# Layer 0's second linear in seven block products, and layer 1's first batch without an opening of its own

## The chip, the core and the metric

The kernel runs on one core of a Trainium2 chip. A core has a matrix engine (TensorE, PE in the profile), three engines for vectors (VectorE or DVE, ScalarE or ACT, GpSimd or POOL) and SyncE (SP), which issues the DMAs here. The engines run side by side, each through its own instructions in order, and wait for one another by semaphores. The metric is the device time of one execution in microseconds, median of several runs.

## The reference, cut to what matters

Two layers follow each other on 16 batches of a 1024 x 256 matrix x, in float32:

```python
# layer 0
agg = einsum('nm,bmd->bnd', A_hat, x)              # A_hat: adj + I, scaled by degrees
h   = relu(batchnorm(agg @ W1.T + b1))             # 512 hidden
out = batchnorm(h @ W2.T + b2)                     # the second linear: 512 -> 256
x   = layernorm(x + out)
# layer 1
c   = mean(x, channels)
Wg  = adj * gate(c_i - c_j)                        # per batch, 1024 x 1024
q   = relu((x.T @ Wg) * para);  k, v = split(x @ kv_w)
x   = layernorm(x + attention(q, k, v))            # 4 heads
```

A batch norm needs the mean and variance over all batches, so the second linear can't start before the first has been through all of them, and layer 1 can't start before the second has.

## The kernel before

**Layer 0, up to the second linear.** For each batch, `aggregate` multiplies x by the scaled adjacency (in batches 1 to 15 by seven products of half-size blocks, after Strassen and Winograd, in which GpSimd makes the sums of blocks of x, `sums_x`), and `hidden` gives the 512 hidden channels of its two halves. A *unit* is one half of a batch (512 rows): 32 units, each a tile `hT` of 128 x 4 x 512. The last `KEEP` = 5 stay in SBUF, the others are written to DRAM. The pool `hp` has 9 such tiles. `bn_affine` turns statistics into a scale and a shift (DVE, with two POOL instructions for the root).

**The second linear** (L340 to L389). Units are taken in the order kept ones first. For each, `first` (L350) is four relus on ScalarE in place, `second` (L356) eight matmuls (two output halves c times four k), then for each c `bn_stats` from PSUM on DVE, a copy to `y` on ScalarE, and a DMA of y to `yT` in DRAM. `fetch` reads units from DRAM four ahead. The weights of layer 1 are loaded behind the sixth unit, in one go.

**Layer 1.** A list `at` holds, for each slot, which pieces are issued there. A batch has NC = 8 slots; its attention is 16 steps, four of which follow every two slots (`scores`, `exps`, `sums`, `attend`). Score tiles have two PSUM buffers, so scores wait for the exps of the step before. The pieces around it prepare later batches: two batches ahead `load`, `bn2` (L436: layer 0's second batch norm applied to yT, ScalarE), `ln1_a` (transposes `py`, add x, statistics), `ln1_b`, `x1_t` (transposes `px`, copy), `means`, `crow` (the means as a row on all partitions); one batch ahead the gate tiles `wg_a` and `wg_b`, `keys`, `values`, and `graph` (the products for the queries `q`). `dens`, `recips`, `finish_a` and `finish_b` normalise and write the output of a batch. `finish_b` waits for `nm` from POOL. `arrange` (L772) sorts the pieces of a slot: `dens` and `bn2` first, the gate in pairs, the long products spread between the short pieces, and whatever isn't an instruction of PE behind what ranks before it in `order` (L758).

**The opening of batch 0** (L802 to L876) isn't in that list. It has buffers of its own for tiles 2 and 3 of the four that make up the batch (taken from the pool `ep`), so that all four are loaded at once; applies bn2 and the statistics to all four; normalises on ScalarE (`ln1_b0`); makes keys of the first half before tiles 2 and 3 are transposed; copies keys on DVE; and makes all four query sums side by side in the score tiles (`graph0`), one gate tile after the other, while batch 1 is prepared in the slots beside it.

**The end.** In the last batch `finish_b` of the first half is put late, behind the last step (L720), r tiles come from the pool of x1 (L648), and `range_all` (a check on the softmax denominators) is in slot NC + 1, before the last `finish_a`.

The line that decides the first places in a slot, and the ranks:

```python
        order = (dens, recips, finish_a, finish_b, x1_t, ln1_a, ln1_b, means, load, crow)
...
            first += [fa for fa in pieces if fa[0] is bn2]
```

Of the kernel before, what the change touches and what calls it, by code (L numbers as in the profile page):

```python
# [16 lines left out]
P = 128  # L17
# [5 lines left out]
def gnn_norm_attention_kernel(  # L23
# [62 lines left out]

    with ExitStack() as l0:
# [6 lines left out]
        KEEP = 5  # L94
# [227 lines left out]
        def load_weights():  # L322
            nc.sync.dma_start(kvw, kv_w.rearrange("(c p) f -> p c f", p=P))
            for i in range(0, NT, 2):
                nc.sync.dma_start(
                    adj_sb[:, i : i + 2, :], adj[i * P : (i + 2) * P, :].rearrange("(c p) m -> p c m", p=P)
                )
            nc.sync.dma_start(para_sb, para.rearrange("o (c p) h w -> p c (o h w)", p=P))

        def load(b, j):  # L330
            yts[b, j] = ldp.tile([P, CT, 2 * P], F32, tag="yt", name=f"yt{b}_{j}")
            xrs[b, j] = ldp.tile([P, 2, C], F32, tag="xr", name=f"xr{b}_{j}")
            fetch_rows(b, j)

        def fetch_rows(b, j):
            nc.sync.dma_start(yts[b, j], yT_dram[b][:, :, ts(j, 2 * P)])
            nc.sync.dma_start(xrs[b, j], x[b, ts(j, 2 * P), :].rearrange("(a p) c -> p a c", p=P))


        with ExitStack() as ph2:  # L340
            yp = ph2.enter_context(tc.tile_pool(name="yp", bufs=3))
            ps = ph2.enter_context(tc.tile_pool(name="ps2", bufs=4, space=PSUM, reuse_waits="tile"))

            order = list(range(len(units) - KEEP, len(units))) + list(range(len(units) - KEEP))

            def fetch(u):
                hT[u] = hp.tile([P, HT, FB], F32, tag="h", name=f"hL{u}")
                nc.sync.dma_start(hT[u], h_dram[u])

            def first(u):  # L350
                for f in range(HT):
                    nc.scalar.activation(
                        hT[u][:, f, :], hT[u][:, f, :], AF.Relu, bias=t1[:, f : f + 1], scale=s1[:, f : f + 1]
                    )

            def second(u):  # L356
                b, h = units[u]
                y = yp.tile([P, CT, FB], F32, tag="y", name=f"y{u}")
                po = [ps.tile([P, FB], F32, tag="a", name="po") for c in range(CT)]
                mm = [(c, k) for c in range(CT) for k in range(HT)]  # L360
                if u == order[0]:
                    mm.sort(key=lambda ck: ck[1])
                for c, k in mm:
                    nc.tensor.matmul(  # L364
                        po[c], W2T[:, k, ts(c, P)], hT[u][:, k, :], start=(k == 0), stop=(k == HT - 1)
                    )
                for c in range(CT):
                    nc.vector.bn_stats(st2[:, c, b * NH + h, :], po[c])  # L368
                    nc.scalar.copy(y[:, c, :], po[c])
                    if u == order[-1]:  # L370
                        bn_affine(st2, c, g2t, be2t, b2t, s2, t2, "bn2")
                nc.sync.dma_start(yT_dram[b][:, :, ts(h, FB)], y)
                hT.pop(u)

            AHEAD = 4
            for u in order[KEEP : KEEP + AHEAD]:
                fetch(u)
            for k in range(len(units) + 1):
                if k < len(units):
                    first(order[k])  # L380
                if k > 0:
                    second(order[k - 1])
                    if KEEP + AHEAD + k - 1 < len(units):
                        fetch(order[KEEP + AHEAD + k - 1])
                if k == KEEP:
                    load_weights()
                if k == len(units) - 2:
                    for j in range(LDP):
                        load(0, j)  # L389

# [22 lines left out]
    def fast():  # L413
      with ExitStack() as fx:
# [102 lines left out]
        def keys(b, c, h):  # L517
            if h == 0:
                kTs[b, c] = kp.tile([P, N], F32, tag="kT", name=f"kT_{b}_{c}")
            p = ps_t.tile([P, FB], F32, tag="t", name="pk")  # L520
            for k in range(CT):
                nc.tensor.matmul(  # L522
                    p, kvw[:, k, ts(c, P)], x1Ts[b][:, k, ts(h, FB)], start=(k == 0), stop=(k == CT - 1)
                )
            (nc.vector.tensor_copy if b == 0 else nc.scalar.copy)(kTs[b, c][:, ts(h, FB)], p)
# [16 lines left out]
        def graph(b, m):  # L542

            h, c, k = m // (CT * NT), m // NT % CT, m % NT
            if k == 0:
                pg[b] = ps_t.tile([P, FB], F32, tag="t", name="pg")
            nc.tensor.matmul(  # L547
                pg[b], x1s[b, k // 2][:, k % 2, ts(c, P)], wgs[b, k][:, ts(h, FB)], start=(k == 0), stop=(k == NT - 1)
            )
            if k == NT - 1:  # L550
                queries(b, c, h, pg[b])

        def queries(b, c, h, p):
            qs = qTs[b, c, h] = qp.tile([P, FB], F32, tag="qT", name=f"qT_{b}_{c}_{h}")
            nc.vector.tensor_mul(qs, p, para_sb[:, c, ts(h, FB)])  # L555
            nc.vector.tensor_scalar(qs, qs, 0.0, scale, op0=OP.max, op1=OP.mult)
# [85 lines left out]
        def finish_a(b, j):  # L642
# [5 lines left out]
            pool_r = (rp, "r") if b < B - 1 else (x1p, "x1")  # L648
            r = pool_r[0].tile([P, 2, C], F32, tag=pool_r[1], name=f"r_{b}_{j}")
# [62 lines left out]
        for b in range(B):  # L712

            for hf in range(NH):
# [3 lines left out]
                for k in range(KB // 2):  # L718
                    put(b, t + 1 + k, finish_a, b, hf * (KB // 2) + k)
                    late = NC - t - 2 - k if b == B - 1 and hf == 0 else 0  # L720
                    put(b, t + 2 + k + late, finish_b, b, hf * (KB // 2) + k)
            if b == 0:
                continue

            put(b - 2, 2, begin, b)
            for j in range(NT // 2):
                put(b - 2, j, load, b, j)
# [25 lines left out]
        put(B - 1, NC + 1, range_all)  # L753
# [4 lines left out]
        order = (dens, recips, finish_a, finish_b, x1_t, ln1_a, ln1_b, means, load, crow)  # L758
# [13 lines left out]
        def arrange(pieces):  # L772
# [3 lines left out]
            first += [fa for fa in pieces if fa[0] is bn2]  # L776
# [24 lines left out]

        def ln1_b0(j):  # L802
            mv, rs = mvs.pop((0, j))
            nm = sm.tile([P, 2], F32, tag="nm", name=f"nm_a{j}")
            for a in range(2):
                nc.gpsimd.tensor_scalar(
                    nm[:, a : a + 1], mv[:, a, 0:1], rs[:, a : a + 1], -1.0, op0=OP.mult, op1=OP.mult
                )
            for a in range(2):
                r = x1s[0, j][:, a, :]  # L810
                i = 2 * j + a
                nc.scalar.activation(
                    r, r, AF.Identity, bias=nm[:, a : a + 1], scale=rs[:, a : a + 1], accum_out=css[0][:, i : i + 1]
                )

        def gate0(i):
            wg_a(0, i)
            wg_b(0, i)

        PG0 = []  # L820

        def graph0(k):
            if k == 0:
                PG0.extend(ps_s.tile([P, 2, FB], F32, tag="s", name=f"pg0_{h}") for h in range(NH))
            for h in range(NH):
                for c in range(CT):
                    nc.tensor.matmul(  # L827
                        PG0[h][:, c, :],
                        x1s[0, k // 2][:, k % 2, ts(c, P)],
                        wgs[0, k][:, ts(h, FB)],  # L830
                        start=(k == 0),
                        stop=(k == NT - 1),
                    )
            if k == NT - 1:
                for h in range(NH):
                    for c in range(CT):
                        queries(0, c, h, PG0[h][:, c, :])

        begin(0)
        for j in range(LDP, NT // 2):  # L840
            t = ep.tile([P, 2, FB], F32, tag="e", name=f"first{j}")
            yts[0, j] = t[:, 0, :].rearrange("p (c n) -> p c n", c=CT)
            xrs[0, j] = t[:, 1, :].rearrange("p (a c) -> p a c", a=2)
            fetch_rows(0, j)
        for f in (bn2, ln1_a):
            for j in range(NT // 2):
                f(0, j)
        ln1_b0(0)
        ln1_b0(1)
        x1_t(0, 0)  # L850
        x1_t(0, 1)
        ln1_b0(2)
        ln1_b0(3)
        for c in range(CT):
            keys(0, c, 0)
        x1_t(0, 2)
        x1_t(0, 3)
        means(0)
        crow(0)
        gate0(0)  # L860
        for c in range(CT):
            keys(0, c, 1)
        gate0(1)
        values(0, 0)
        values(0, 2)
        gate0(2)
        values(0, 4)
        values(0, 6)

        def opening(s):  # L870

            k = s + NC
            if 0 <= k < NC:
                for i in range(3 + 2 * k, min(5 + 2 * k, NT)):
                    gate0(i)
                graph0(k)  # L876

        NK = NT // 2  # L880
        for t in range(min(at) // 2, max(max(at) // 2, nsteps // NK - 1) + 1):
            g = NK * t
            now = [p for s in (2 * t, 2 * t + 1) for p in [(opening, (s,))] + arrange(at.get(s, []))]
# [175 lines left out]
```

## Time and profile before

| | us |
|---|---|
| median of 3 runs | 2610.95 (2610.77 to 2611.19) |
| the profiled execution, its time | 2610.95 |
| its span, first to last instruction | 2609.2 |
| layer 0 up to the second linear | 0 to 635 |
| second linear, PE | 635.3 to 857.8 |
| from there to the first scores | 857.8 to 925.2 |
| one batch of layer 1 (scores to scores) | 106.9 |
| the last matmul's start | 2598.0 |

| engine | busy us | share of the span |
|---|---|---|
| PE | 2551.5 | 98% |
| DVE | 1425.5 | 55% |
| ACT | 1217.5 | 47% |
| POOL | 364.0 | 14% |

The profile is of one execution. A line of a timeline gives start, duration, engine, line of the kernel, operation, what it writes and reads, shapes, how many instructions were merged (x), and in brackets how long the engine was idle before and what ended that. A float32 matmul is two instructions in it. A line of the busy time by stretch gives, for each engine, the time in which it ran anything.

### The profile page before, as it was taken

What the parts mean: (1) busy time and instruction counts of PE and PEld (TensorE: products, weight loads), DVE (VectorE), ACT (ScalarE), POOL (GpSimd) and SP (SyncE); (2) the same over time, 40 slices, a digit from 0 to 9 for tenths busy, and PEclk for the clock granted to TensorE, in tenths of its full rate; (3) what the DMA queues carried; (4) which work ended last, traced back from release to release, by engine and by line L of the source; (5) the groups of instructions that cost most, each with busy time, mean ns of one, the idle gap of its engine ahead of it and who ended that gap; (6) DMA issues with size and microseconds to landing.
All of it is one profiled execution on the core that took longest, in us unless ns stands there. A gap on an engine that the chain in (4) does not pass through costs nothing.

```text
span 2609.2 us, 32969 instructions
## 1 busy us (share of the span) xinstructions
PE 2551.5 (98%) x13177; PEld 1117.1 (43%) x13177; DVE 1425.5 (55%) x2250; ACT 1217.5 (47%) x1647; POOL 364.0 (14%) x472
## 2 busy tenths in 40 slices
PE   8999999999999899999999999999999999999997
PEld 4444444444444444444444444444444444443432
DVE  5222222223222465867758667676576775867666
ACT  2111111113555564564655646556465574664644
POOL 1111110100000100211102201111021110211112
PEclk9999999999999899999999999999999999999998
DMA  3222222221863211011000100111000111011000
GB/s 129 81 81 81 97 81 81 81 109 43 315 234 129 81 41 33 25 44 46 25 33 28 55 33 25 34 33 50 33 25 33 34 49 33 25 41 33 9 9 26
DMA packets 93824, 161.65 MB, mean 62 GB/s; under 512 B 7656, under 2 KB 73824, under 8 KB 86752
## 3 DMA queue, kind: packets, MB, share of 16 engines
q1 hardware_dynamic: 93664, 159.48, 17.4%
q8 instruction: 105, 1.72, 0.3%
q14 instruction: 55, 0.45, 0.1%
HBM read 97.53 MB, written 61.93 MB: 61 GB/s over the span
## 4 chain that ended last, share of the span: by engine, by line
PE 91%; ACT 3%; DVE 3%; issue 1%; DMA 1%; POOL 1%; SPq 0%; ACTq 0%; POOLq 0%; DVEq 0%
PE s L573 17%; PE o L604 17%; PE pa L263 14%; PE pg L547 14%; PE po L364 8%; PE ph L284 8%; PE pk L522 4%; PE pv L533 2%; PE pd L625 1%; PE px L472 1%; PE pa L247 1%; PE pg L827 1%; PE pf L647 1%; ACT wg L509 1%; ACT wg L510 1%
## 5 line engine op out<-in xcount | busy, mean ns | idle before, releaser
L585 ACT ACTIVATE e<-s 128x1024 f32<-128x1024 f32 x512 | 496.5, 1021 | 398.7 <-PE s L573 347.2
L594 DVE TENSOR_TENSOR acc<-acc,e 128x1024 f32<-128x1024 f32 x384 | 470.7, 1226 | 88.3 <-ACT e L585 58.6
L573 PE MATMUL s<-qT,kT 64*64 64x512 f32 x4096 | 490.9, 594 | 5.5 <-ACT e L585 4.7
L604 PE MATMUL o<-e,v 64*64 64x512 f32 x4096 | 485.3, 589 | 0.0
L547 PE MATMUL pg<-wg,x 128*128 128x512 f32 x960 | 441.1, 594 | 12.3 <-DVE wg L514 12.3
L303 ACT COPY hT<-ph 128x512 f32<-128x512 f32 x128 | 74.9, 586 | 453.8 <-PE ph L284 453.8
L604 PEld LDWEIGHTS o<-e,v 64*64 64x64 f32 x4096 | 156.7, 133 | 283.5 <-issue 278.5
L573 PEld LDWEIGHTS s<-qT,kT 64*64 64x64 f32 x4096 | 149.8, 133 | 294.8 <-issue 271.2
L547 PEld LDWEIGHTS pg<-wg,x 128*128 128x128 f32 x960 | 168.9, 190 | 176.1 <-issue 149.1
L514 DVE SCALAR_TENSOR_TENSOR wg<-wg,adj_sb 128x1024 f32<-128x1024 f32 x128 | 156.8, 1225 | 127.7 <-ACT wg L510 125.5
L284 PE MATMUL ph<-agg,W1T 128*128 128x512 f32 x512 | 222.2, 592 | 0.0
L66 POOL TENSOR_SCALAR rs_z<-mv_z 128x2 f32<-128x2 f32 x64 | 41.1, 642 | 1036.5 <-DVE mv_z L405 1006.9
L364 PE MATMUL po<-hL,W2T 128*128 128x512 f32 x432 | 185.6, 592 | 0.0
L304 DVE BATCH_NORM_STATS2 st<-ph 128x6 f32<-128x512 f32 x128 | 89.5, 699 | 136.6 <-ACT hT L303 136.6
L263 PE MATMUL pa<-T,sx 128*128 128x512 f32 x360 | 156.9, 592 | 0.0
L284 PEld LDWEIGHTS ph<-agg,W1T 128*128 128x128 f32 x512 | 97.3, 190 | 122.5 <-issue 122.2
L368 DVE BATCH_NORM_STATS2 st<-po 128x6 f32<-128x512 f32 x64 | 44.7, 699 | 169.4 <-PE po L364 169.4
L364 PEld LDWEIGHTS po<-hL,W2T 128*128 128x128 f32 x432 | 82.1, 190 | 103.3 <-issue 103.3
L473 ACT COPY x1T<-px 128x512 f32<-128x512 f32 x64 | 37.1, 581 | 178.5 <-PE px L472 178.5
L533 PE MATMUL pv<-kvw,x1T 128*128 128x256 f32 x512 | 120.1, 379 | 0.0
L522 PE MATMUL pk<-x1T,kvw 128*128 128x512 f32 x256 | 119.0, 609 | 0.7 <-ACT x1T L473 0.7
L555 DVE TENSOR_TENSOR qT<-pg,para_sb 128x512 f32<-128x512 f32 x64 | 43.8, 684 | 128.1 <-PE pg L547 127.1
(144 smaller groups left out, 2619.7 us busy)
## 6 DMA issues: line engine op xcount, KB each, us to landing
h<-hT SPq DMA_DIRECT2D x27, 1024.0 KB, 3.8
hL<-h SPq DMA_DIRECT2D x27, 1024.0 KB, 8.6
x<-in_x_dram SPq DMA_DIRECT2D x16, 1024.0 KB, 5.0
yT<-y SPq DMA_DIRECT2D x32, 512.0 KB, 3.7
out_dram<-r SPq DMA_DIRECT2D x64, 256.0 KB, 2.1
yt<-yT SPq DMA_DIRECT2D x62, 256.0 KB, 3.0
xr<-in_x_dram SPq DMA_DIRECT2D x62, 256.0 KB, 5.0
crow<-crow_d SPq DMA_DIRECT2D x15, 512.0 KB, 4.0
```

The source lines that it names most:

```text
L263: nc.tensor.matmul(p, w[:, k, :], m[:, k, :], start=(k == 0), stop=(k == KN - 1))
L284: nc.tensor.matmul(p, W1T[:, k, ts(f, P)], aggT[b][:, k, ts(h, FB)], start=(k == 0), stop=(k == CT - 1),)
L304: nc.vector.bn_stats(st1[:, f, u, :], p)
L364: nc.tensor.matmul(po[c], W2T[:, k, ts(c, P)], hT[u][:, k, :], start=(k == 0), stop=(k == HT - 1))
L514: nc.vector.scalar_tensor_tensor(t, t, 1.0, adj_sb[:, i, :], op0=OP.add, op1=OP.mult)
L522: nc.tensor.matmul(p, kvw[:, k, ts(c, P)], x1Ts[b][:, k, ts(h, FB)], start=(k == 0), stop=(k == CT - 1))
L533: nc.tensor.matmul(p[:, ts(a, C)], x1Ts[b][:, k, ts(j + a, P)], kvw[:, k, C:], start=(k == 0), stop=(k == CT - 1),)
L547: nc.tensor.matmul(pg[b], x1s[b, k // 2][:, k % 2, ts(c, P)], wgs[b, k][:, ts(h, FB)], start=(k == 0), stop=(k == NT - 1))
L573: nc.tensor.matmul(t[r * HD : (r + 1) * HD, h, :], kTs[b, pair][h * HD : (h + 1) * HD, ts(2 * cb + r, HD)], qTs[b, pair, hf][h * HD : (h + ...
L585: nc.scalar.activation(E[g, a], S.pop((g, a)), AF.Exp)
L594: nc.vector.tensor_add(ACC[b, hf, pair], ACC[b, hf, pair], E[g, a])
L604: nc.tensor.matmul(O[b, hf, pair][r][h * HD : (h + 1) * HD, :], vs[b][r * HD : (r + 1) * HD, cb, pair * P + h * HD : pair * P + (h + 1) * HD],
```

## The change

The second linear is now made for two batches side by side, each by seven products of half-size blocks. With the weights in blocks of (output half, k half) and the hidden units in blocks of (k half, unit), the four sums of weight blocks are made once (`SV`, POOL), and the sums of h blocks in place: one on DVE, three on POOL between the products that read the old value and those that read the new. A generator `seven` issues one product of a batch at a time, and the two batches' generators alternate. What leaves PSUM goes through the running sums u and v: one ScalarE copy and seven DVE additions for a batch, and `bn_stats` reads y in SBUF. The relus of all four kept units are issued before the first product; those of the next pair's units come behind the third to sixth product of a pair. Fetches are for a whole pair, at its start. `KEEP` is 4, PSUM has 8 buffers here, and the weights of layer 1 are loaded over five pairs.

Batch 0 of layer 1 goes through the list `at` like the others: `continue` for b == 0 is gone, only its first two tiles are loaded ahead, and the whole opening is removed. So are the special cases of batch 0's key copies and of the last batch (late `finish_b`, r tiles from x1's pool); `range_all` is one slot later; and `bn2` isn't put first in its slot, but ranks behind `means`.

```diff
+    def seven(product, u, v, out, done=lambda i, j: None):
+        nc.scalar.copy(u, product(1))
+        yield
+        nc.vector.tensor_add(out[0][0], product(2), u)
+        done(0, 0)
+        yield
+        nc.vector.tensor_add(u, product(6), u)
+        yield
+        nc.vector.tensor_add(v, product(7), u)
+        yield
+        nc.vector.tensor_add(out[1][0], product(4), v)
+        done(1, 0)
+        yield
+        p = product(5)
+        nc.vector.tensor_add(out[1][1], p, v)
+        nc.vector.tensor_add(u, p, u)
+        done(1, 1)
+        yield
+        nc.vector.tensor_add(out[0][1], product(3), u)
+        done(0, 1)
+        yield
...
-        KEEP = 5
+        KEEP = 4
...
+            def second(b, final):
+                unit = [b * NH + h for h in range(NH)]
+                (b00, b01), (b10, b11) = ([hT[u][:, i * KF : (i + 1) * KF, :] for u in unit] for i in range(2))
+                bs = {1: b00, 2: b10, 3: b11, 4: b10, 5: b01, 6: b00, 7: b01}
+                nc.vector.tensor_sub(b01, b11, b01)
...
+                def product(n):
+                    p = ps.tile([P, FB], F32, tag="a", name="po")
+                    for k in range(KF):
+                        nc.tensor.matmul(p, ws[n][:, k, :], bs[n][:, k, :], start=(k == 0), stop=(k == KF - 1))
+                    return p
+
+                def done(c, h):
+                    nc.vector.bn_stats(st2[:, c, b * NH + h, :], ys[h][:, c, :])
+                    if final and (c, h) in ((1, 1), (0, 1)):
+                        bn_affine(st2, c, g2t, be2t, b2t, s2, t2, "bn2")
...
+                for k, _ in enumerate(seven(product, u, v, out_q, done)):
+                    if k == 0:
+                        nc.gpsimd.tensor_add(b00, b00, b01)
+                    if k == 1:
+                        nc.gpsimd.tensor_sub(b10, b10, b00)
+                    if k == 3:
+                        nc.gpsimd.tensor_sub(b01, b11, b00)
+                    if k >= 5:
+                        nc.sync.dma_start(yT_dram[b][:, :, ts(k - 5, FB)], ys[k - 5])
...
+            for b in pairs[0]:
+                for h in range(NH):
+                    first(b * NH + h)
+            for k, pair in enumerate(pairs):
+                ahead = [b * NH + h for b in pairs[k + 1] for h in range(NH)] if k + 1 < len(pairs) else []
+                for u in ahead:
+                    fetch(u)
+                load_weights(k)
...
+                gens = [second(b, not ahead and b == pair[-1]) for b in pair]
+                for n in range(7):
+                    for g in gens:
+                        next(g)
+                    if 2 <= n and ahead:
+                        first(ahead.pop(0))
...
-            pool_r = (rp, "r") if b < B - 1 else (x1p, "x1")
-            r = pool_r[0].tile([P, 2, C], F32, tag=pool_r[1], name=f"r_{b}_{j}")
+            r = rp.tile([P, 2, C], F32, tag="r", name=f"r_{b}_{j}")
...
-                    late = NC - t - 2 - k if b == B - 1 and hf == 0 else 0
-                    put(b, t + 2 + k + late, finish_b, b, hf * (KB // 2) + k)
-            if b == 0:
-                continue
+                    put(b, t + 2 + k, finish_b, b, hf * (KB // 2) + k)
...
-        put(B - 1, NC + 1, range_all)
+        put(B - 1, NC + 2, range_all)
...
-        order = (dens, recips, finish_a, finish_b, x1_t, ln1_a, ln1_b, means, load, crow)
+        order = (dens, recips, finish_a, finish_b, x1_t, ln1_a, ln1_b, means, bn2, load, crow)
...
-            first += [fa for fa in pieces if fa[0] is bn2]
...
-        def ln1_b0(j):
...
-        def opening(s):
...
-            now = [p for s in (2 * t, 2 * t + 1) for p in [(opening, (s,))] + arrange(at.get(s, []))]
+            now = arrange(at.get(2 * t, [])) + arrange(at.get(2 * t + 1, []))
```

## The prediction

> **The bound.** The views were read in this order: the page, whose part 1 has PE busy in 98% of the span; the busy time by stretch, to see where the 2% is; and the timelines of PE, ACT, DVE and POOL in one batch of layer 1 and in the tail. By stretch:
>
> ```profile
> core 0: us, PE busy (x) PEld busy (x) DVE busy (x) ACT busy (x) POOL busy (x), PEclk, DMA share, GB/s
> ...
> 672.00:857.70 185.70, 185.70 (x433) 81.89 (x431) 39.45 (x59) 104.98 (x158) 0.79 (x2) 1.00 0.61 222
> 857.70:942.20 84.50, 73.17 (x266) 38.62 (x265) 45.97 (x97) 47.59 (x78) 10.79 (x26) 0.88 0.20 63
> ...
> 1124.90:1231.80 106.90, 105.95 (x701) 45.81 (x705) 73.29 (x116) 61.60 (x79) 17.53 (x24) 1.00 0.11 36
> ```
>
> PE never rests in the second linear (first line), rests 11 us in the opening of layer 1 (second), and 0.95 us in each 106.9 us batch (third). So a matmul saved in the second linear is worth its full price, and anything that makes PE wait once in a batch is paid about fifteen times. The price of a matmul: the chain of waits gives 500 of the instructions of L364 in 214.87 us, 0.4297 us each (two to a matmul).
>
> The batch is tight at two places. ScalarE there (start, duration, line):
>
> ```profile
> 1252.53 1.15 ACT L505 ACTIVATE wg<-crow,hcs 128x1024 f32<-128x1024 f32 x1
> 1253.58 1.08 ACT L439 ACTIVATE yt<-yt,t,s 128x256 f32<-128x256 f32 x2
> 1254.56 0.57 ACT L525 COPY kT<-pk 128x512 f32<-128x512 f32 x1
> 1255.93 0.58 ACT L540 COPY v<-pv 128x512 f32<-128x512 f32 x1 [0.80 <-PE pv L533]
> 1256.41 1.15 ACT L509 ACTIVATE wg<-crow,cs 128x1024 f32<-128x1024 f32 x1
> ...
> 1260.08 1.92 ACT L585 ACTIVATE e<-s 128x1024 f32<-128x1024 f32 x2
> ...
> 1272.47 1.09 ACT L439 ACTIVATE yt<-yt,t,s 128x256 f32<-128x256 f32 x2
> 1273.47 1.08 ACT L668 ACTIVATE r<-r,nm,rs_z 128x256 f32<-128x256 f32 x2
> 1274.45 0.56 ACT L540 COPY v<-pv 128x512 f32<-128x512 f32 x1
> 1274.91 1.15 ACT L509 ACTIVATE wg<-crow,cs 128x1024 f32<-128x1024 f32 x1
> ```
>
> bn2 (L439) of the first tile stands in a gap that ends with a wait of 0.80 for PE; the exps at 1260.08 start with no wait. PE beside it:
>
> ```profile
> 1261.47 1.90 PE L573 MATMUL s<-qT,kT 64*64 64x512 f32 x16
> ...
> 1276.27 0.60 PE L449 MATMUL py<-ident,yt 128*128 128x128 f32 x4
> 1276.71 4.46 PE L547 MATMUL pg<-wg,x 128*128 128x512 f32 x10
> 1282.11 1.12 PE L547 MATMUL pg<-wg,x 128*128 128x512 f32 x2 [0.95 <-DVE wg L514]
> ```
>
> And in the tail, where no graph product covers a late normalisation, a wait of ACT for POOL stops PE:
>
> ```profile
> 2549.89 3.56 PE L573 MATMUL s<-qT,kT 64*64 64x512 f32 x16 [4.13 <-ACT e L585]
> ```
>
> **The skill.** The Trainium skill, "SBUF — State Buffer", Who interferes with whom: a VectorE instruction with two SBUF inputs and a GpSimd instruction that reads SBUF exclude each other[...]. The trace agrees: L66 on POOL takes 0.22 us at 1276.45 with DVE idle, 1.66 at 1262.54 under L591. The Trainium skill, "TensorE: Matmul & The Clock Gate", What's actually happening: after idling the array runs at half rate until it has been busy for a few us. The trace: 8 instructions of L522 take 6.11 us at 875.77, 3.44 at 883.83.
>
> **The change.** The order of instructions on each engine is that of the changed program; durations are from rows of the kernel before.
>
> *Stage 2, PE.* Seven products of 2 matmuls for eight, so 64 of 512 instructions go: 64 x 0.4297 = 27.5 us. 448 take 192.2.
>
> *Stage 2, start.* Before, the matmuls follow the relus one by one: by 642.9 us 12 are done, and 500 follow without a break. In the changed order all 16 relus of the first two batches precede the first copy, and PE alternates batches. Relu 4 starts at 642.03 and each takes 0.705 (5 in 3.63), so the third unit's first two are done at 642.03 + 7 x 0.705 = 647.0. B1 waits for this from 638.5: PE is cold by then (+2.5 us, from L522's pair above). B's subtraction needs relu 16 (651.2) and 1.23 us (L594's shape), then B's first POOL sum. POOL's 128x512 sums start every 1.22 us (L233 to L236), so a 128x1024 sum is taken as 2.4; the Trainium skill's "GPSIMD Engine Reference", Elementwise — side-by-side cycle accounting, has 4497 ns for 2048 elements, an estimate of 2.25. B6 then starts at about 655.9, and the 14 products end at 671.4, 2.5 us of cold clock included. The other 392 instructions: 168.4. End 839.8, where before it was 857.8.
>
> *Stage 2, later pairs.* A pair takes 24.05 us of PE. ACT has 16 relus and 2 copies (12.5), DVE 2 subtractions, 14 additions at 0.62 from start to start and 8 bn_stats at 0.7 (16.7), POOL 6 sums (14.4), DMA 4 MB of h, 2 of y and 1 of weights, 17 us at the 415 GB/s that 692 to 696 us shows. All fit. What is near is POOL's order: VectorE ends the last pair's work 1.7 us into the pair, subtracts for A to 2.9 and for B to 4.0, which blocks A's sum to 4.0 (two SBUF inputs); A's ends at 6.4 (A6 due at 6.9), B's at 8.8 (B6 due at 8.6). I take 0.2 us a pair, 1 us in all; from below 0 (2.25 us a sum), from above 3.5 us a pair, if bn_stats blocked POOL too. Stage 2 ends at 840.8: 17.0 earlier.
>
> *Opening.* Its length, from the end of the second linear to the first key product of batch 1 (927.97), was 70.2. In the changed order:
> bn2's coefficients: VectorE's last four products cost 2 x (2 x 0.62 + 0.7) and 2 x (0.62 + 0.7), and two affines of 2.4 stand among them; it is 3.9 us behind when the last affine starts. Ready at 6.3 instead of 3.2 us.
> Tiles 2 and 3 have no buffers of their own: their loads wait for py of tiles 0 and 1 (8.4, 9.4 us) and for the additions (9.2, 11.0); xr takes up to 5.0 us to land, so tile 2's addition comes at 15.0. Then, a tile at a time: statistics 1.1, ln1_b 0.95, px about 1 at the cold clock. px of tile 3 ends at 24.5, crow at 26.3.
> Keys from there: cold, the first copy at 29.4, and behind it all of ACT's gate work: 8 tiles of 1.05 or 2.15 us, key and value copies, bn2 of batch 1. wg 7 leaves ACT at 50.8 and VectorE at 54.4, so the first query sum is done at 55.3.
> Three more sums: 48 x 0.43 = 20.6, and 2.3 of transposes. First score at 78.2, keys of batch 1 at 80.0.
> So +9.8 us. From below +5 (early loads, warm clock), from above +15.
>
> *bn2 in the batches.* It is no longer put first in its slot. Tile 0's goes from the gap at 1253.58 to behind wg 2: wg 2 still starts at 1256.41, and the exps at 1261.06 instead of 1260.08. The next scores (PE 1261.47) need the buffer that the first exp reads until 1262.08: PE waits 0.7. Tile 1's goes from 1272.47 to behind r, v and wg 4: v still waits for pv (1274.4), wg 4 ends at 1277.0, bn2 at 1278.1. py (1276.27) waits 1.9; the 12 graph instructions take 5.15 from 1278.6 and find wg 5 ready (1281.7), so the 0.95 goes; the scores come at 1283.95 instead of 1283.17, 0.8. Tiles 2 and 3 have time: py at 1301.99 and 1308.89. Together 1.45 us in each of the 13 windows 1 to 13 (in window 0 no output work is ahead of it): +18.9. From below 0, from above 2 a window.
>
> *Tail.* The output normalisations of the last batch's first half run in slots 6 and 7 again, ahead of exps: ACT waits for POOL's nm as at 2547.84 (4.65), PE as above: 4.5 and 1.7 of cold clock, 6.2 less a fraction: +6.0. The range check goes behind the last tile: pf no longer waits for it, and the last addition starts at 2597.4 instead of 2599.16: -1.8. Together +4.2.
>
> Sum on the span: 2609.2 - 17.0 + 9.8 + 18.9 + 4.2 = 2625.1. The profiled execution took 2610.95, 1.75 more than its span, and is the median of the runs. Forecast 2626.9.
>
> **Rivals.**
> *The batches absorb the later bn2* (not slower): ACT idles 45 us in a batch's 106.9, and a wait of 0.7 could vanish if scores had buffers to spare. Against: there are two, and the timeline leaves 0.3 us. Then 18.9 goes: 2608.0. It decides from under 0.5 us a window on.
> *POOL bounds the pairs*: if every VectorE instruction that reads SBUF blocked it, POOL would have 14.4 + 8.1 of 24 us, with waits between that don't overlap; 3.5 us in each of 7 pairs: 2651. Against: POOL's sums of phase 1 all take 1.26 to 1.27 with VectorE's PSUM additions beside them.
> *The opening is longer*, its chain cold throughout, +16 for +9.8: 2633.
> That the products aren't what bounds stage 2 is excluded by the first line above.
>
> **Numbers.** Chances: forecast 0.62, absorbed 0.15, POOL 0.11, opening 0.12. The forecast's own bounds are about 8 us to each side; that is 2619 to 2635; the range reaches over the longer opening and to the middle of the absorbed case, 2608 to 2640, and leaves out POOL and the other half of that case, under 2 in 10. A measurement here can tell 0.2%, 5.2 us. Faster by more: a third of the absorbed case, 0.05. Within: half of it and the forecast's low edge, 0.11. Slower: 0.84.
>
> **The test.** PE's 448 instructions of the second linear ending near 841, with one gap of 8 us at its start; first scores about 78 us later; scores periods of 108.4 where they were 106.9, with waits of PE for e (0.7) and of py for yt (1.9); a second PE wait of about 4.5 us for e, 20 us before the end. It is wrong if the period stays under 107.4, or if pairs last over 25 us.

## The result, and the profile after

The changed kernel takes 2627.26 us (median of 4 runs, 2626.8 to 2628.35), the kernel before 2611.07 beside it: ratio 1.0063, 95% interval 1.0045 to 1.0080. It is 16.2 us slower. The profiled execution took 2627.65 us, its span is 2625.8, 16.6 more than before.

The busy time by stretch, for the changed kernel, with the engines' columns as before:

```profile
core 0: us, PE busy (x) PEld busy (x) DVE busy (x) ACT busy (x) POOL busy (x), PEclk, DMA share, GB/s
671.42:839.70 168.28, 168.28 (x393) 73.84 (x391) 118.41 (x170) 76.55 (x110) 103.81 (x43) 1.00 0.72 278
839.70:922.41 82.71, 62.34 (x202) 33.32 (x201) 42.73 (x108) 31.54 (x48) 11.32 (x20) 0.81 0.17 57
1120.19:1228.40 108.21, 106.44 (x702) 45.69 (x704) 73.32 (x116) 61.94 (x79) 16.35 (x24) 1.00 0.11 35
```

The seven pairs after the first (first line) have no gap in PE at all, 24.03 us a pair. The opening, from the last product to the first key product of batch 1 (second line), is 82.7 us where it was 70.2, with 20 us of rest in it. A batch (third line) lasts 108.21 us for 106.93, with 1.77 us of rest for 0.95.

PE at the start of stage 2:

```profile
634.78 1.12 PE L407 MATMUL po<-hT,W2T 128*128 128x512 f32 x2 [1.39 <-ACT hT L393]
636.23 1.13 PE L407 MATMUL po<-hT,W2T 128*128 128x512 f32 x2 [0.32 <-ACT hT L393]
647.02 7.40 PE L407 MATMUL po<-hT,W2T 128*128 128x512 f32 x12 [9.66 <-ACT hT L393]
```

After the wait of 9.66 us for the relus it runs through to 839.7, 18.0 us before the old end. Half a microsecond of that is not the change's: layer 0 ended earlier in this execution, as the first product of the kernel before shows:

```profile
635.29 3.70 PE L364 MATMUL po<-hT,W2T 128*128 128x512 f32 x8 [1.39 <-ACT hT L352]
```

From its first product (634.78 for 635.29) to its last, the second linear is 17.4 us shorter. The pairs had hardly any time to spare on POOL, though; its sums in one pair:

```profile
674.30 5.53 POOL L419 TENSOR_TENSOR hL<-hL,hL 128x1024 f32<-128x1024 f32 x2 [9.36 <-PE po L407]
679.77 4.70 POOL L421 TENSOR_TENSOR hL<-hL 128x1024 f32<-128x1024 f32 x2
684.41 4.69 POOL L423 TENSOR_TENSOR hL<-hL,hL 128x1024 f32<-128x1024 f32 x2
```

The pair began at 671.42, a product lasts 1.717 us, so the second batch's product 6, the sixth product of the pair, is due at 680.0, and its sum (the second of L419) ends at 679.8.

PE in a batch, at the two places where bn2 comes later:

```profile
1258.75 2.00 PE L629 MATMUL s<-qT,kT 64*64 64x512 f32 x16 [0.47 <-ACT e L641]
...
1274.95 0.33 PE L507 MATMUL py<-ident,yt 128*128 128x128 f32 x1 [1.14 <-ACT yt L497]
1275.44 0.55 PE L507 MATMUL py<-ident,yt 128*128 128x128 f32 x3 [0.16 <-ACT yt L497]
1275.83 5.32 PE L606 MATMUL pg<-wg,x 128*128 128x512 f32 x12
```

A wait for e that wasn't there, waits of py for yt that weren't there, and 12 graph instructions that no longer wait for a gate. In the tail there is now a second stop; ScalarE first, PE below:

```profile
2596.75 1.09 ACT L723 ACTIVATE r<-r,nm,rs_z 128x256 f32<-128x256 f32 x2 [4.71 <-POOL nm L715]
2597.75 1.91 ACT L641 ACTIVATE e<-s 128x1024 f32<-128x1024 f32 x2
```

```profile
2598.80 3.69 PE L629 MATMUL s<-qT,kT 64*64 64x512 f32 x16 [4.20 <-ACT e L641]
2602.27 2.49 PE L660 MATMUL o<-e,v 64*64 64x512 f32 x16
```

The exp stands behind an activation that waits for POOL, and PE behind the exp.

By stretch, against before: stage 2 -18.0, opening +12.5, batches +16.2 (from batch 1's keys to the first stop in the tail), tail +5.9: +16.6.

### The profile page after: what moved, and what is told of

It is laid out like the page before. It is cut to its first block, busy times and chain, and to the rows that moved or that the text cites. A ratio compares the mean times of both kernels' runs of the same rounds, so it can differ in the third digit from the quotient of the medians.

```text
span 2625.8 us, 33112 instructions
## 1 busy us (share of the span) xinstructions
PE 2535.9 (97%) x13113; PEld 1104.1 (42%) x13113; DVE 1518.8 (58%) x2390; ACT 1191.2 (45%) x1587; POOL 467.0 (18%) x516
## 4 chain that ended last, share of the span: by engine, by line
PE 89%; ACT 4%; DVE 4%; issue 2%; POOL 1%; DMA 0%; SPq 0%; ACTq 0%; POOLq 0%; DVEq 0%
PE pg L606 16%; PE s L629 16%; PE o L660 16%; PE pa L291 14%; PE ph L312 8%; PE po L407 7%; PE pk L580 4%; PE pv L591 1%; PE pd L681 1%; PE px L530 1%; PE pa L275 1%; PE py L507 1%; ACT yt L497 1%; ACT wg L567 1%; PE pf L703 1%
## 5 line engine op out<-in xcount | busy, mean ns | idle before, releaser
L606 PE MATMUL pg<-wg,x 128*128 128x512 f32 x1024 | 469.8, 596 | 1.8 <-DVE wg L572 1.3
L606 PEld LDWEIGHTS pg<-wg,x 128*128 128x128 f32 x1024 | 182.2, 191 | 175.1 <-issue 167.3
L66 POOL TENSOR_SCALAR rs_z<-mv_z 128x2 f32<-128x2 f32 x64 | 41.0, 641 | 1048.0 <-DVE mv_z L463 1026.0
L66 POOL TENSOR_SCALAR rs_a<-mv_a 128x2 f32<-128x2 f32 x64 | 51.7, 808 | 444.5 <-DVE mv_a L463 444.5
L672 DVE TENSOR_TENSOR ot<-o,ot 128x512 f32<-128x512 f32 x64 | 44.2, 691 | 135.7 <-ACT ot L671 134.2
L591 PE MATMUL pv<-kvw,x1T 128*128 128x256 f32 x512 | 120.2, 379 | 0.0
L291 PE MATMUL pa<-AhT,x 128*128 128x512 f32 x240 | 105.4, 592 | 0.0
```

Source lines behind the costliest of these rows:

```text
L66: nc.gpsimd.tensor_scalar(dst, src, add, None, op0=OP.add)
L291: nc.tensor.matmul(p, w[:, k, :], m[:, k, :], start=(k == 0), stop=(k == KN - 1))
L591: nc.tensor.matmul(p[:, ts(a, C)], x1Ts[b][:, k, ts(j + a, P)], kvw[:, k, C:], start=(k == 0), stop=(k == CT - 1),)
L606: nc.tensor.matmul(pg[b], x1s[b, k // 2][:, k % 2, ts(c, P)], wgs[b, k][:, ts(h, FB)], start=(k == 0), stop=(k == NT - 1))
```

## The experiments

Each kernel below was timed beside the kernel before on the same chip; the ratio is to that one. Kernel n is the kernel of experiment n. In the four sets of runs, the result's among them, the kernel before had medians of 2611.07 to 2612.06, so a difference between kernels of two sets is good to about 1 us.

**1. bn2 first again** (against the changed kernel)

```diff
-        order = (dens, recips, finish_a, finish_b, x1_t, ln1_a, ln1_b, means, bn2, load, crow)
+        order = (dens, recips, finish_a, finish_b, x1_t, ln1_a, ln1_b, means, load, crow)
+            first += [fa for fa in pieces if fa[0] is bn2]
```

> The changed kernel with one thing put back: bn2 of a tile stands first in its slot again, ahead of sums and conversions. Theory (the batch period grew from 106.93 to 108.21 us because yt comes 0.6 us later to ScalarE and so e and py come later to TensorE, in slots 0 and 2): the period goes back to about 106.9 us, 13 windows give some -16.5 us, and the time is about 2611 us; TensorE's waits for e ahead of group (0,1)'s scores and for yt ahead of py in group (2,3) are as in the kernel before (none and 0.95 us before the scores). Rival (the period grew from something else that moved, such as the new load and keys order or the ScalarE key copies): the period stays near 108.2 us and the time near 2627 us.

2609.93 us (2607.96 to 2612.54), ratio 0.9996 (0.9988 to 1.0005): 17.3 us less. The busy time of one of its batches, then PE in it:

```profile
1120.00:1226.93 106.93, 105.98 (x705) 45.84 (x701) 73.30 (x117) 61.62 (x79) 17.14 (x24) 1.00 0.11 37
```

```profile
1268.76 4.46 PE L606 MATMUL pg<-wg,x 128*128 128x512 f32 x10
1274.16 1.12 PE L606 MATMUL pg<-wg,x 128*128 128x512 f32 x2 [0.94 <-DVE wg L572]
```

The period is 106.93 again, in all 13 windows, and the wait for the gate is back in its place. The new loads, key copies and the rest of the list cost the batches nothing.

**2. Only tile 0's bn2 first**

```diff
+            first += [fa for fa in pieces if fa[0] is bn2 and fa[1][1] == 0]
```

> The changed kernel with bn2 of tile 0 alone first in its slot; those of tiles 1 to 3 stay ranked. Theory (two places lose time in each of 13 windows: TensorE's wait for e in group (0,1), 0.57 us, from tile 0; py waiting for yt in group (2,3), 0.71 us net, from tiles 1 and 2): period 107.64 us, the first wait gone and the second as changed, 7.4 us less, about 2620 us. Rival (it is tile 0's lateness that carries into group (2,3) too): about 2611 us, as with all four tiles first. Rival (the two overlap, one wait takes over from the other): under 2 us.

2617.73 us (2614.01 to 2619.3), ratio 1.0021 (1.0013 to 1.0028): 9.5 us less. In its PE timeline the wait for e is gone and this one is unchanged:

```profile
1273.62 0.33 PE L507 MATMUL py<-ident,yt 128*128 128x128 f32 x1 [1.14 <-ACT yt L497]
```

The period is 107.45 (1107.20 to 1214.65, from one graph product to the same one of the next batch). So the two places add up, but as 0.76 and 0.52 us a window, not 0.57 and 0.71. The 0.57 was read from the bracket and the longer matmul; from the products before the stop (o at 1256.38) to those after it (1260.57) PE needs 4.19 us for 3.43: 0.76.

**3. The late finish of the last batch again**

```diff
-            r = rp.tile([P, 2, C], F32, tag="r", name=f"r_{b}_{j}")
+            pool_r = (rp, "r") if b < B - 1 else (x1p, "x1")
+            r = pool_r[0].tile([P, 2, C], F32, tag=pool_r[1], name=f"r_{b}_{j}")
...
-                    put(b, t + 2 + k, finish_b, b, hf * (KB // 2) + k)
+                    late = NC - t - 2 - k if b == B - 1 and hf == 0 else 0
+                    put(b, t + 2 + k + late, finish_b, b, hf * (KB // 2) + k)
```

> The changed kernel with one thing put back: the last batch's first-half layer-norm finish is put to the slots after all its scores, with r tiles from x1's pool. Theory (its tail is 5.9 us longer because ScalarE's activation waits for POOL's nm ahead of an exp, a second TensorE wait of 4.2 us with some 2 us of cold clock behind it): the second wait goes, the span from the last batch's first stall on is shorter by 6 to 6.7 us, and the time is about 2621 us. Rival (the finish only moved work that must be done anyway, and the end after the last matmul grows by what the middle gains): within 2 us of the changed kernel, near 2627 us.

2622.24 us (2620.34 to 2623.61), ratio 1.0041 (1.0028 to 1.0055): 5.0 us less, the span 6.1 less. PE at the place of the second stop:

```profile
2590.76 1.95 PE L629 MATMUL s<-qT,kT 64*64 64x512 f32 x16
2592.53 1.90 PE L660 MATMUL o<-e,v 64*64 64x512 f32 x16
2594.24 1.90 PE L629 MATMUL s<-qT,kT 64*64 64x512 f32 x16
```

From the scores before the stop to the last `pd` it is 12.2 us (2590.76 to 2602.94) for 18.9 (2590.94 to 2609.84): 6.7 gained. From there to the end it is 16.8 for 16.0: 0.8 given back, the rival's share.

**4. The hand-made opening again.** The opening of before, its buffers and its key copies put back; bn2 in the batches and the tail stay as changed.

```diff
+            if b == 0:
+                continue
...
+        begin(0)
+        for j in range(LDP, NT // 2):
+            t = ep.tile([P, 2, FB], F32, tag="e", name=f"first{j}")
...
+            now = [p for s in (2 * t, 2 * t + 1) for p in [(opening, (s,))] + arrange(at.get(s, []))]
```

> The changed kernel with the opening for the first batch put back (its order by hand, own buffers for tiles 2 and 3, key copies on VectorE, all four query sums at once), and bn2 in the batches and the tail as changed. Theory: of the 12.5 us by which batch 1's keys come later after the last product, some 3.1 us belong to the seven products themselves (the norm's coefficients are ready 6.3 us after the last product instead of 3.2), and the opening is worth the other 9.4 us: batch 1's keys about 73 us after the last product instead of 82.7, and the time about 2618 us. Rival (the batches take up a later start, since they wait for POOL or ScalarE anyway): less than 3 us, near 2625 us.

2618.12 us (2616.55 to 2619.03), ratio 1.0024 (1.0014 to 1.0034): 9.1 us less. From its last product to batch 1's keys, busy time by stretch:

```profile
841.38:914.63 73.25, 58.83 (x201) 31.57 (x201) 41.66 (x96) 34.60 (x60) 11.32 (x27) 0.84 0.18 58
```

73.25 us for 82.7, and 3.1 more than in the kernel before: the part that the seven products themselves cost. What of the opening brings the 9 us is tried in part in experiments 9 and 10.

**5. The seven products alone**: the kernel before with the new stage 2 and nothing else of the change (`KEEP`, `load_weights`, `seven`, `second` as changed; opening, bn2, tail as before).

> The kernel before with the second linear by seven products alone; opening, bn2 first and the late finish stay. Theory: stage 2 ends 18 us earlier, the norm's coefficients come 3.1 us later after it, all else stays: 2611.1 - 18.0 + 3.1 = about 2596 us. Rival (what the three other edits cost is not additive, or the sums made in place slow the opening's loads): 2600 us or more.

2597.97 us (2595.86 to 2598.68), ratio 0.9946 (0.9932 to 0.9959): 13.6 us faster than the kernel before beside it (2611.56), 29.3 faster than the whole change. The three restorations above take 31.4 us off the changed kernel; with the 1.8 us of the moved range check, which kernel 5 lacks, 29.6 was due. The parts add up. The theory's 2596 was 2 us low, and the rival's 2600 as much too high: the theory took 18.0 us from the changed kernel's profile. In this kernel's profile the second linear takes 205.5 us from its first product to its last, for 222.5 before (-17.0), and from there to batch 1's keys it is 73.6 us for 70.2 (+3.4), which is -13.6.

**6. POOL's third sum twice**

```diff
                     if k == 3:
                         nc.gpsimd.tensor_sub(b01, b11, b00)
+                        nc.gpsimd.tensor_sub(b01, b11, b00)
```

> The changed kernel with the last of POOL's three sums of a batch issued twice (2.35 us each, the second writes the same block again). Theory (POOL's sums hide behind TensorE's products, but with little room in their places: in the pair from 671.4 us on the first sum of the second batch ends 0.2 us before its product, the third some 1.2 us before its own): two more sums a pair make the second batch's product 5 wait 3.5 us, 8 pairs, 28 us, about 2655 us, which is the time that the rival of a POOL-bound pair gave. Rival (POOL is busy some 15 of a pair's 24 us, so 4.7 us more still fit): no change, 2627 us.

2661.2 us (2660.03 to 2661.91), ratio 1.0191 (1.0175 to 1.0206): 33.9 us more. PE in one pair and in a later one:

```profile
693.93 1.98 PE L407 MATMUL po<-hL,SV 128*128 128x512 f32 x4 [0.53 <-POOL hL L424]
698.68 5.42 PE L407 MATMUL po<-hL,SV 128*128 128x512 f32 x12 [2.76 <-POOL hL L424]
...
726.54 7.11 PE L407 MATMUL po<-hL,SV 128*128 128x512 f32 x12 [2.76 <-POOL hL L424]
```

A wait of 2.76 in every pair, and one of about 0.5 in all but the first; with what hangs on them 3.8 us (a pair lasts 27.86, from 676.07 to 703.93), about 30 us for eight. In two pairs the 12 instructions after the wait take 7.11 for 5.42, the rest. So the changed kernel stands just this side of a bound by POOL: busy 15 of 24 us, and no room for 2.35 more a batch. The room that this experiment used up is the one before product 5 (1.2 us in the second batch); the 0.2 us before product 6 are read from the trace of the changed kernel, and no run tests them.

**7. Relus column by column** (against kernel 5)

```diff
-            for b in pairs[0]:
-                for h in range(NH):
-                    first(b * NH + h)
+            for f in range(HT):
+                for b in pairs[0]:
+                    for h in range(NH):
+                        first(b * NH + h, (f,))
```

> The kernel with the seven products alone, and one order changed in it: the relus of the four kept units are issued column by column (f0 of all four, then f1, f2, f3), not unit by unit. Theory (product 1 of the second batch waits 9.7 us behind the last coefficients' relus of the first two units, and all of the first pair's start is late by that): the third product of the first batch starts near 648 us instead of 654.3, stage 2 ends 4 to 6 us earlier, about 2593 us. Rival (the sums in place on VectorE and POOL, which need the last column, set the start anyway): within 1 us of 2598 us.

2592.02 us (2591.18 to 2594.06), ratio 0.9927 (0.9914 to 0.9941): 6.0 us less than kernel 5, from which it differs by 4.8 us in the second linear (200.7 us from first product to last for 205.5). PE at its start:

```profile
637.57 5.26 PE L410 MATMUL po<-hT,W2T 128*128 128x512 f32 x8 [1.69 <-ACT hT L396]
643.43 2.84 PE L410 MATMUL po<-hT,W2T 128*128 128x512 f32 x6 [0.60 <-ACT hT L396]
647.88 1.98 PE L410 MATMUL po<-hT,SV 128*128 128x512 f32 x4 [1.60 <-POOL hT L422]
651.46 5.42 PE L410 MATMUL po<-hT,SV 128*128 128x512 f32 x12 [1.60 <-POOL hT L422]
```

The third product (the first with SV) starts at 647.9; what remains are two waits of 1.60 for POOL.

**8. Weight sums on VectorE, range check one slot later** (against kernel 7)

```diff
-            nc.gpsimd.tensor_add(SV[:, 0], wq[1][0], wq[1][1])
+            nc.vector.tensor_add(SV[:, 0], wq[1][0], wq[1][1])
...
-        put(B - 1, NC + 1, range_all)
+        put(B - 1, NC + 2, range_all)
```

> As the kernel with column-wise relus, and two things more: the four sums of weight blocks on VectorE instead of POOL (they run beside VectorE's last two coefficient operations, which took 0.74 and 0.76 us there instead of 0.16 and 0.22), and the range check's sum put one slot later as in the changed kernel. Theory: the last coefficients come 1.1 us earlier, of which column-wise relus leave 0.2 to 1 us, and the end after the last matmuls is 1.8 us shorter: about 2590.5 us. Rival: neither lies on the path any more, 2593 us.

2590.77 us (2590.39 to 2592.17), ratio 0.9921 (0.9908 to 0.9935). Time alone doesn't tell it from kernel 7. VectorE's last coefficient operations, in kernel 7 and then here:

```profile
640.98 0.74 DVE L139 TENSOR_TENSOR s<-rs_bn,g1t 128x1 f32<-128x1 f32 x1 [0.61 <-POOL rs_bn L68]
641.76 0.77 DVE L140 SCALAR_TENSOR_TENSOR t<-mu_bn,s,be1t 128x1 f32<-128x1 f32 x1
```

```profile
641.27 0.16 DVE L139 TENSOR_TENSOR s<-rs_bn,g1t 128x1 f32<-128x1 f32 x1 [0.61 <-POOL rs_bn L68]
641.47 0.22 DVE L140 SCALAR_TENSOR_TENSOR t<-mu_bn,s,be1t 128x1 f32<-128x1 f32 x1
```

In kernel 7 they end 0.02 us after POOL's first and second sum of weight blocks (641.70 and 642.51); here POOL has no such sum. The 1.1 us are real, and from the first product to the third 0.23 of them is left (12.90 us for 13.13). The end after the last `pd` is 16.0 us for 17.2, 1.1 less and not 1.8.

**9. Own buffers for tiles 2 and 3** (against the changed kernel; loaded ahead into tiles of the pool `ep`)

```diff
-                if b > 0 or j >= LDP:
+                if b > 0:
                     put(b - 2, j, load, b, j)
...
+        for j in range(LDP, NT // 2):
+            t = ep.tile([P, 2, FB], F32, tag="e", name=f"first{j}")
```

> The changed kernel with one part of the old opening put back: tiles 2 and 3 of the first batch have their own buffers and are loaded ahead, not when tile 0's and 1's buffers come free. Theory (ScalarE waits 3.2 us for tile 2's load, and px of tiles 2 and 3 come one after the other behind it, so the means and all gates of the first batch are late): crow about 4 to 5 us earlier, of which the graph products keep 3 to 4 us, since they wait for the gates and for the next batch's tiles: about 2623.5 us. Rival (the next batch's tiles alone, through px in program order, set the first scores): under 1.5 us.

2627.11 us (2626.06 to 2628.99), ratio 1.0059 (1.0046 to 1.0073): no change. PE:

```profile
851.77 1.12 PE L530 MATMUL px<-ident,x 128*128 128x128 f32 x4 [3.18 <-DVE x L516]
852.68 1.06 PE L507 MATMUL py<-ident,first 128*128 128x128 f32 x4
856.20 1.09 PE L530 MATMUL px<-ident,x 128*128 128x128 f32 x4 [2.46 <-DVE x L516]
```

py of tile 2 stands in PE's queue behind px of tile 0, which waits 3.18 us for VectorE here and in the changed kernel; there the later load had landed and bn2 was done (852.4) before py's turn came (853.1). So crow comes 19.3 us after the first py in both kernels. Both my theory and the place I gave the rival were off: by these traces it is the order of the queue that sets the means and gates, though no run changes that order alone.

**10. Key copies of batch 0 on VectorE** (against the changed kernel)

```diff
-            nc.scalar.copy(kTs[b, c][:, ts(h, FB)], p)
+            (nc.vector.tensor_copy if b == 0 else nc.scalar.copy)(kTs[b, c][:, ts(h, FB)], p)
```

> The changed kernel with one part of the old opening put back: VectorE, not ScalarE, copies the first batch's keys. Theory (ScalarE sets the gates' pace from crow on, without a break; its four copies are 2.3 us of it): the eighth gate leaves VectorE up to 2.3 us earlier, and the first scores 1 to 2 us, about 2625.5 us. Rival (the graph products wait for px of the next batch, whose path runs over VectorE, and VectorE gets the copies): no change or up to 1 us slower.

2626.18 us (2624.9 to 2626.64), ratio 1.0053 (1.0039 to 1.0067): 1.1 us less, within what two such medians can differ by. The profile looks better than that: from the first py to batch 1's keys 72.7 us for 75.8. But 2.65 of these 3.05 are one line, here in the changed kernel, then in this one:

```profile
890.94 5.49 PE L606 MATMUL pg<-wg,x 128*128 128x512 f32 x6 [0.64 <-DVE wg L572]
```

```profile
892.48 2.84 PE L606 MATMUL pg<-wg,x 128*128 128x512 f32 x6 [0.73 <-DVE wg L572]
```

The same six instructions behind nearly the same waits, at half the clock in one execution and not in the other (PEclk 0.50 and 1.00 over them). Over all seven profiles with this opening, four have about 5.49 (the changed kernel, 2, 3, 9) and three 2.84 (1, 6, 10). The edits don't sort them: kernels 1 and 2, with waits of 0.69 and 0.74 and of 0.70 and 0.74 there, fall on different sides. Some 0.4 us are left for the copies, and the eighth gate leaves VectorE 44.1 us after the first py for 44.3, not 2.3 us earlier. So ScalarE's copies did not set the gates' pace, and what is left is nearer the rival. Of the opening's 9 us, experiments 9 and 10 account for about 1 at most; how the rest divides between the order of its pieces and the four query sums side by side, no run separates.

**11. The second norm's chains side by side** (against kernel 8): `bn_affine` is a generator with a `yield` ahead of `mu` and ahead of `s`.

```diff
-                    if final and (c, h) in ((1, 1), (0, 1)):
-                        bn_affine(st2, c, g2t, be2t, b2t, s2, t2, "bn2")
+                    if final and (c, h) == (0, 1):
+                        halves = [bn_affine(st2, c_, g2t, be2t, b2t, s2, t2, "bn2") for c_ in range(CT)]
+                        for _ in range(3):
+                            for g in halves:
+                                next(g, None)
```

> The fastest kernel so far (seven products, column-wise relus, weight sums on VectorE, range check one slot later) with the second norm's two coefficient chains run side by side behind the last product, not the first of them ahead of the last product's additions. Theory (VectorE is full from the last six products on, and the first chain stands 2.35 us in front of the last additions, 0.6 us of it only waiting for POOL): the coefficients are ready 1.3 us earlier, about 4.9 us after the last product instead of 6.3, and the time is 2589.5 us. Rival (ScalarE's wait for the loads or for the y stores sets the start of the opening): no change, 2590.8 us.

2589.15 us (2588.43 to 2590.09), ratio 0.9912 (0.9898 to 0.9925). PE's first line of layer 1:

```profile
841.89 0.48 PE L517 MATMUL py<-ident,yt 128*128 128x128 f32 x1 [4.89 <-ACT yt L507]
```

It starts 4.89 us after the last product for 6.84 in kernel 8, since its first transpose needs the coefficients of output half 0 alone, which now come first of the two and came last in kernel 8; the last coefficient comes at 4.8 us for 6.2, and batch 1's keys 71.2 us after the last product for 72.4. Time alone doesn't tell it from kernel 8 (the intervals overlap). It has the lowest median of all: 22.3 us under the kernel before beside it, 38.1 under the changed one.

## Why the prediction was right, step by step

The forecast was 2626.9, the result 2627.26, and the mechanisms are those named, save one in the opening. Four terms were off by 1 to 3 us each, with opposite signs: opening and tail were 4.4 us longer than forecast, stage 2 and the batches 3.7 us shorter. That the sum is within 1 us is luck.

*Stage 2, end.* -17.0 forecast, -18.0 measured. The term that was off is POOL's stall of 0.2 us a pair, 1 us in all: I had the second batch's sum end 8.8 us into a pair and its product due at 8.6; it ends at 8.4. The sum takes 2.35 to 2.37 us where VectorE doesn't hold it, for the 2.4 taken from the 128x512 row. The start comes at the forecast times, second batch's product at 647.02 (647.0) and 14 products done at 671.4 (671.4), but two things cancel in them: layer 0 ended 0.5 us earlier in this execution, and the start itself took 0.5 us longer (12.2 us from the first product to the second batch's, 11.7 forecast). The gap of PE was 9.7 us for the 8 of the test. Experiment 7 shows what that order of relus costs, 5 to 6 us. (The 192.2 us for 448 instructions should read 192.5; the sum does not use it.)

*Opening.* +9.8 forecast, +12.5 measured. The coefficients come at 6.3 us as forecast, and experiment 4 confirms their 3.1 us. Tile 2's addition at 14.5 (15.0), crow at 26.3 (26.3). After that two errors of opposite sign: the last gate left VectorE at 51.2 (54.4), and the four query sums took 29.6 us from there to the first scores where the forecast has 23.8. The working has them unbroken; in the trace px and graph products of the same queue wait for VectorE's `ln1_b` of batch 1 and for gates (0.64 to 1.36 us at a time), and behind one such wait the clock is low for 2.65 us. In the executions where it isn't, the two errors cancel and the opening is close to the forecast: in kernel 1, 79.9 us from the last product to the keys, +9.7. The reason given for tile 2's lateness, its load, was wrong in part (experiment 9): without the load the order of PE's queue gives the same.

*bn2 in the batches.* +18.9 forecast (1.45 us in 13 windows), 16.2 measured (1.28 in each of these 13, 16.6, and 0.4 less in window 0). Right in both places and in kind: the wait for the buffer of e, 0.7 forecast and 0.76 measured; py, 0.8 forecast and 0.52 measured. There py waits 1.14 and 0.16 us, not 1.9, since its first transpose needs only the first half of yt; that the 12 graph instructions then find their gates ready was forecast. The period of 108.21, and experiment 1, which brings back 106.93, exclude the rival that the batches absorb it.

*Tail.* +4.2 forecast, +5.9 measured. The second stop costs 6.7 (6.0 forecast) and stands 27 us before the end, not 20; the range check gives 1.8 (1.8; in experiment 8, 1.1). The remaining 1.1 is the first stop, which was there before: behind the same wait of 4.13 us the 32 instructions take 5.45 us in the kernel before and 6.51 in this execution, at a granted clock of 0.68 and 0.56. That is the clock, not the change: kernels 7, 8 and 11 keep the tail of before at this place and take 6.64, 6.65 and 5.17.

*POOL bounds the pairs* did not come about. Its ground, that every VectorE instruction that reads SBUF blocks POOL, doesn't hold: in the 7 pairs POOL's second and third sums took 2.35 to 2.38 us each, with VectorE's additions from PSUM and bn_stats beside them; only the first sum, under a subtraction with two SBUF inputs, took up to 3.21. But the room is small (0.2 us before product 6), and experiment 6 shows what a POOL-bound pair costs, 34 us in all.

What each part of the change does is now plain: its main part is worth 13.6 us, and each of its three removals takes more than it looks: 17 us for a rank in a list, 9 for an opening, 5 for the place of one layer norm.

## What to carry to other kernels

Where PE runs without rest, cost an edit in two parts: what it takes off PE's queue, once, and what it makes PE wait for, times the number of rounds; 1.28 us in a round took back nearly all that an eighth fewer matmuls had saved in a stage (16.2 us against 17.4). A busy share doesn't tell whether an engine fits: POOL at 15 of 24 us had 0.2 us of room, read from when its result is due. And before a difference between two profiles is put down to an edit, look whether the same instructions behind the same waits ran at another clock.

## What the runs showed of the chip that was not expected

- The clock's price behind a wait varies between executions. Behind the tail's first stop (4.1 us) 32 instructions that take 3.8 us warm took 5.2 to 6.7 in the profiles of this study; behind waits of 0.6 to 1.2 us in the opening, six took 2.84 or 5.49; behind 2.76 us, twelve took 5.42 in six pairs and 7.11 in two. The Trainium skill, "TensorE: Matmul & The Clock Gate", What's actually happening, has a window that runs freely and a count of slow matmuls that differs from run to run, which agrees; it puts the fall to the slow state after an idle window of about 3.4 us, and here waits of 1.15, 0.70 and 0.64 us within 4.5 us, or a single one of 2.76, were at times enough.
- VectorE operations on one element a partition are not safe from POOL: 0.16 and 0.22 us alone, 0.74 and 0.77 beside POOL's 128x256 sums (experiment 8). The rule of the Trainium skill, "SBUF — State Buffer", Who interferes with whom, covers it, since L139 and L140 read two SBUF inputs; each ended 0.02 us after the POOL sum of 0.72 or 0.73 us that started within 0.02 us of it.
- One SBUF input can hold POOL too. The kernel before, where the prediction reads L66 of 1.66 us as lying under L591:

```profile
1262.37 1.19 DVE L591 TENSOR_TENSOR acc<-e,e 128x1024 f32<-128x1024 f32 x1
1262.54 1.66 POOL L66 TENSOR_SCALAR rs_z<-mv_z 128x2 f32<-128x2 f32 x1 [38.53 <-DVE mv_z L405]
1263.47 0.69 DVE L507 TENSOR_SCALAR wg<-wg 128x1024 int32<-128x1024 int32 x1
```

  L591 ended at 1263.56; L66 went on to 1264.20, 0.04 us after L507, which reads one tensor. So it is in 14 batches. Under L591 without L507 behind it L66 took 1.02 us (from 1284.03), under L507 alone 0.56 (from 1280.31). The same section of the Trainium skill frees one SBUF input only "outside the 2-port perf modes"; whether L507 runs in such a mode, no view here says. The forecast did not depend on it: VectorE has no such instruction in the second linear.
